# Pacing interleaved layer-0/1 steps by weights instead of by count, in a four-layer fp32 kernel

## The chip, the cores and the metric

The kernel runs on one core of a Trainium2 chip. The metric is the device time of one execution in microseconds (us), as the median of several runs. One further execution was recorded by the hardware profiler; all durations below are from that one.

## What is computed

The input is x of 16 batches, each 256 rows by 256 channels. Four layers are added to it one after the other (`x = x + layer(x)`), all in float32. Cut to what matters:

```python
# layer 0: gated exponential averages over the rows, 16 decays, then a gate, a product and a layer norm
ctx = causal_ema(x, tau_ctx)
gated = x * sigmoid(concat(x, ctx) @ Wg.T + bg)
mod = 0.5 + sigmoid(gelu(x @ Wn1.T + bn1) @ Wn2.T + bn2)         # one column per decay d
temporal = sum_d softmax(blend)[d] * causal_ema(gated * mod[d], tau_raws[d])
out = (gelu(x @ Wsoma.T + bsoma) * sigmoid(temporal @ Wtemp.T + btemp)) @ Wout.T
x = x + layernorm(out) * gamma + beta
# layer 1: masked softmax pooling over the rows
scores = tanh(x @ W1 + b1) @ v
x = x + (softmax(mask(scores)) @ x) / count
# layer 2: 8 experts and a shared one, every batch through all nine, hidden width 1024
x = x + sum_e coef[b, e] * ((silu(x @ Wg[e]) * (x @ Wu[e])) @ Wd[e])
# layer 3: an MLP of hidden width 1024 whose last 64 columns come from one of 8 experts
x = x + concat(gelu(x @ W1 + b1) @ W2 + b2, gelu(x @ W1 + b1) @ We[idx] + be[idx])
```

Matrix products keep float32 accuracy by splitting each operand into a rounded part and a low part, and adding three products: high x high, high x low, low x high (`mm3`, lines 95 to 98).

## The kernel before

**Layers 2 and 3 are the plan.** Lines 693 to 716 write a list `plan` of 640 units, of which 576 are layer-2 units and 64 are layer-3 units. A layer-2 unit (`l2_unit`, line 608) takes one chunk of 128 hidden columns of one expert for a pair of batches (512 columns), or two chunks for one batch (256 columns each). It does the products into pg and pu, Silu on ScalarE (line 595), the product with pu on VectorE (line 596), rounding on ScalarE and the low part on GpSimd (`hidden`), and two units later the product back into y (LAG is 2). Batch 0 goes alone through the first five experts (units 0 to 19), batch 1 joins at unit 20, batches 2 and 3 board at unit 56, and the later pairs at units 128, 200, 288, 360, 448 and 520. A layer-3 unit (`l3_chunk`, line 649) is shorter. In the planner's time, `at`, a layer-2 unit counts 4 and a layer-3 unit 3.

**Weights.** `prefetch` runs one load per chunk ahead, ten chunks at most (RING). The first two times that a chunk is used it comes raw from DRAM into one of two buffers (`raws`), ScalarE rounds it (line 542), VectorE or GpSimd makes the low part (line 544), and then the raw buffer is free for the next load. In the first five experts every third low part is GpSimd's, later all are VectorE's. From the third use on, the ready pair is read back from DRAM. All loads are issued in order by SyncE's queue.

**Layers 0 and 1 are woven in.** Each batch passes through two generators, which stop at each `yield`. `traces` (line 245) has 21 steps for a batch after the first:
- steps 0 to 3: the splits of x and the context scan; the small products; `mod` written to DRAM; and the gate (24 matmuls of 256 columns into a buffer of tag "ps", then two tanh)
- steps 4 to 19: one step for each of the 16 decays d (a "d-step" below): two products on VectorE (line 352), two scans on VectorE (line 356) and the sum into `tacc` on GpSimd (line 360); each second one loads two rows of `mod` (line 347). Step 9 also holds `soma`, 12 matmuls and two Gelu
- step 20: the split of the sum

`pooled` (line 385) has 10 steps: the gate on the traces (0), its product (1), the product with Wout and the norm (2, 3), transposes and the splits (4), scores (5, 6), the softmax (7), transposes of it (8), and the product pp with the sum into `acc` (9, lines 492 to 504). It is one serial chain over all engines. Outside batch 0, every product of both generators goes through the one buffer of tag "ps" in PSUM, so their order in the program is their order in time.

**The order.** `phases` (lines 740 to 753) says which generators run beside each other: pooled(b) beside traces(b+1). For b = 0 and odd b only FRONT = 4 steps of traces(b+1) are beside pooled(b), and the rest follows in a phase of its own. `feed` interleaves the generators of a phase in proportion to their steps. `due` (line 802) lists for each pair when its steps must be done (SLACK = 16 of `at` before it boards, about four units) and how many steps, `ready`, that is. After each unit, `pace` gives the steps per unit of `at` that meet the most urgent due time, `rate` is that times the unit's length, and lines 834 to 840 run as many whole steps as are owed. No step runs ahead of the first three units of a layer-3 group. Each step is placed behind the unit's product on VectorE and its last matmul (`step`, line 807); the program's compiler then orders each engine's queue by this order and by what it expects to be ready.

Of the kernel before, what the change touches and what calls it, by code (L numbers as in the profile page):

```python
# [19 lines left out]
ND = 16  # L20
# [3 lines left out]
FRONT = 4  # L24
# [5 lines left out]
LAG = 2  # L30
BOOST = 400
HOLD = 3
STEPS = {"traces": 21, "pooled": 10}
FIRST = 13
ALONE = 5
NEG = -1e30
# [8 lines left out]
def fused_kernel(  # L45
# [55 lines left out]
    def load_x(b):  # L101
        xr = xin.tile([P, 2, S], F32, tag="xr", name=f"xr{b}")
        nc.sync.dma_start(xr, xT[b])
        return xr

    def load_xt(b):
        xt = xin.tile([P, 2, S], F32, tag="xt", name=f"xt{b}", bufs=1)
        nc.sync.dma_start(xt, x[b])
        return xt
# [133 lines left out]
    held, last_of = {}, {}  # L243
# [364 lines left out]
    def l2_unit(pos, cis, bs):  # L608


        uid[0] += 1
        u = uid[0]
        n = S * len(bs)
        p = bs[0] // 2
        off = (bs[0] % 2) * S
        xt = x2_tiles[p]
        sl = slice(off, off + n)
        parts = [(ci, ring_tiles["e", pos, ci], slice(i * n, (i + 1) * n)) for i, ci in enumerate(cis)]
        pg = ps_gu.tile([P, 512], F32, tag="gu", name=f"pg_{u}")
        pu = ps_gu.tile([P, 512], F32, tag="gu", name=f"pu_{u}")  # L620
        for q, o in ((pg, 0), (pu, 256)):
            for _, w, cs in parts:
                for k in range(2):
                    ws = slice(o + k * P, o + (k + 1) * P)
                    mm3(q[:, cs], w[:, 0, ws], w[:, 1, ws], xt[:, 0, k, sl], xt[:, 1, k, sl], k == 0, k == 1)
        t = hidden(pg, pu, u)
        e = cis[0] // NF

        def down():
            if cis[0] % NF == 0:  # L630
                y_of[0] = [ps_y.tile([P, 512], F32, tag=f"y{m}", name=f"y{m}_{u}") for m in range(2)]
            for m in range(2):
                ws = slice(512 + m * P, 512 + (m + 1) * P)
                for ci, w, cs in parts:
                    mm3(
                        y_of[0][m][:, :n], w[:, 0, ws], w[:, 1, ws], t[:, 0, cs], t[:, 1, cs],
                        ci % NF == 0, ci % NF == NF - 1,
                    )
            if cis[-1] % NF == NF - 1:
                for m in range(2):  # L640
                    for i, b in enumerate(bs):
                        a = acc_of(b)[:, m]
                        V.scalar_tensor_tensor(  # L643
                            a, y_of[0][m][:, i * S : (i + 1) * S], coef[:, b, e : e + 1], a, ALU.mult, ALU.add
                        )
                if p in ends.get(pos, []) and bs[-1] % 2:
                    leaving.append(p)

        st2.push(down)

    def l3_chunk(p, f):
        uid[0] += 1
        xt = x2_tiles[p]
        w = ring_tiles[("f", p, f)]
        q = ps_gu.tile([P, 512], F32, tag="gu", name=f"q_{uid[0]}")
        for k in range(2):
            ws = slice(k * P, (k + 1) * P)
            mm3(q, w[:, 0, ws], w[:, 1, ws], xt[:, 0, k], xt[:, 1, k], k == 0, k == 1)
        t = hidden(q, None, uid[0], bias=vec[:, V_L3B1 + f : V_L3B1 + f + 1])
        u = uid[0]  # L660

        def down():
            if f == 0:
                y_of[0] = [ps_y.tile([P, 512], F32, tag=f"y{m}", name=f"z{m}_{u}") for m in range(2)]
            mm3(y_of[0][0], w[:, 0, 256:384], w[:, 1, 256:384], t[:, 0], t[:, 1], f == 0, f == NF - 1)
            for i in range(2):
                b = 2 * p + i
                cw = ring_tiles[("c", b, f // 4)]
                ws = slice((f % 4) * P, (f % 4 + 1) * P)
                ts = slice(i * S, (i + 1) * S)  # L670
                mm3(
                    y_of[0][1][:, ts], cw[:, 0, ws], cw[:, 1, ws], t[:, 0, ts], t[:, 1, ts],
                    f == 0 and i == 0, f == NF - 1 and i == 1, skip_group_check=True,
                )
            if f == NF - 1:
                a = acc_tiles[p]
                V.scalar_tensor_tensor(a[:, 0], y_of[0][0], vec[:, V_B2 : V_B2 + 1], a[:, 0], ALU.add, ALU.add)  # L677
                nc.sync.dma_start(out[p, :, 0], a[:, 0])
                for i in range(2):
                    b = 2 * p + i  # L680
                    ts = slice(i * S, (i + 1) * S)
                    V.scalar_tensor_tensor(  # L682
                        a[:, 1, ts], y_of[0][1][:, ts], bias3[:, b : b + 1], a[:, 1, ts], ALU.add, ALU.add
                    )
                nc.sync.dma_start(out[p, :, 1], a[:, 1])

        st2.push(down)
# [48 lines left out]

    n_done, n_steps = [0], [0]
    phases, alone, ready = [[(traces, 0)]], {}, []  # L740
    count = FIRST
    for b in range(NB):
        more = b + 1 < NB
        phases.append([(pooled, b)] + [(traces, b + 1)] * more)
        count += STEPS["pooled"]
        if more and (b == 0 or b % 2):
            alone[len(phases) - 1] = FRONT
            phases.append([(traces, b + 1)])
            ready.append(count + FRONT)
            count += STEPS["traces"]  # L750
        else:
            count += STEPS["traces"] * more
            ready.append(count)

    def feed():
        gens, left = {}, {}
        for i, phase in enumerate(phases):
            for f, b in phase:
                if f is traces and 0 < b + 1 < NB and b + 1 not in asked:
                    asked.add(b + 1)  # L760
                    xin_tiles[b + 1] = load_x(b + 1)
                    xt_tiles[b + 1] = load_xt(b + 1)
                if (f, b) not in gens:
                    gens[f, b] = f(b, b == 0)
                    left[f, b] = FIRST if (f, b) == (traces, 0) else STEPS[f.__name__]
            todo = {k: left[k] for k in phase}
            if i in alone:
                todo[phase[1]] = alone[i]
            total = sum(todo.values())
            share = {k: n / total for k, n in todo.items()}  # L770
            owed = dict.fromkeys(phase, 0.0)
            live = set(phase)
            while live:
                for k in phase:
                    owed[k] += share[k]
                k = max((k for k in phase if k in live), key=lambda k: owed[k])
                owed[k] -= 1
                todo[k] -= 1
                left[k] -= 1
                n_steps[0] += 1  # L780
                next(gens[k])
                if todo[k] == 0:
                    live.discard(k)
                if left[k] == 0:
                    assert next(gens[k], gens) is gens
                    n_done[0] += k[0] is pooled
                yield

    asked = set()
    steps = feed()  # L790
    while n_steps[0] < FIRST:
        next(steps)
# [6 lines left out]
    at = [0]  # L799
# [4 lines left out]
    def pace(t, s):  # L804
        return max([(s1 - s) / max(t1 - t, 1) for t1, s1 in due if s1 > s] or [1.0])

    def step():


        if "h" not in last_of:  # L810
            return next(steps, None)
        with tc.issue_after(last_of["h"].ins), tc.issue_after(last_of["pe"].ins):
            return next(steps, None)

    def leave():
        while leaving:
            split_x3(leaving.pop())

    owed = 0.0
    for i, item in enumerate(plan):  # L820
        kind, args, _, done = item[:4]
        if kind == "l2":
            bs = args[2]
            while n_done[0] <= bs[-1]:
                step()
            l2_unit(*args)
        else:
            if args[0] not in x3_done:
                st2.flush()
                leave()  # L830
            l3_chunk(*args)
        leave()

        rate = pace(at[i], n_steps[0]) * item[4]
        owed += rate
        soon = plan[min(i + 1, len(plan) - 1)]
        if not (soon[0] == "l3" and soon[1][1] < HOLD):
            for _ in range(min(int(owed), int(rate) + 2)):
                step()
                owed -= 1  # L840
        prefetch(len(done))
    st2.flush()

# [108 lines left out]
```

## Time and profile before

| | |
|---|---|
| median of 3 runs | 2860.03 us (2858.63 to 2860.83) |
| the profiled execution | 2858.32 us |
| its span, first to last instruction | 2856.1 us |
| TensorE busy (matmuls) | 2783.3 us, 97% |
| VectorE busy | 1440.9 us, 50% |
| GpSimd busy | 1294.4 us, 45% |
| ScalarE busy | 1238.7 us, 43% |

The profile's page shows busy time by engine, the span in 40 slices, and the costliest groups of instructions. In its lines, PE is TensorE, DVE VectorE, ACT ScalarE, POOL GpSimd, SP SyncE; "L352" is line 352 of the kernel; a group reads "output tile <- input tiles, shape, count". A view of waits names who waited, at which tile and line, for whom, with the sum, the count and the longest. A helper's line (L93 for a low part, L86 for a rounding on ScalarE, L96 to L98 for the three products) is shared by many tiles, so those groups are told apart by their tiles. Batch 0's layers 0 and 1 take the first 68 us; unit 0 starts at 68 us, and unit 56's first product at 402.65 us.

### The profile page before, as it was taken

Reading aid. Unit: us, or ns where it says so; the run is one execution under the profiler, and the core shown is the slowest. Engines: PE = TensorE matmul, PEld = TensorE weight load, DVE = VectorE, ACT = ScalarE, POOL = GpSimd, SP = SyncE. Lnnn points to the kernel's source line nnn. Section 1 sums busy time; section 2 is a strip of 40 time slices with the busy share of each in tenths; the row PEclk is TensorE's granted clock in tenths of the full one; section 3 lists DMA queues with packets and bytes.
Section 4 is the critical chain, followed back from the end, with each engine's and each line's share of the span. In section 5 each row is a group of like instructions: output and inputs, shape, how many; then the busy total and the mean of one; then the engine's idle time right before and its main releaser. Section 6 shows DMA issues by size and latency. Waiting matters only on the chain. (4 is left out here: it accounts for less than half of the span.)

```text
span 2856.1 us, 36960 instructions
## 1 busy us (share of the span) xinstructions
PE 2783.3 (97%) x13632; PEld 2338.7 (82%) x13632; DVE 1440.9 (50%) x2664; ACT 1238.7 (43%) x2054; POOL 1294.4 (45%) x981
## 2 busy tenths in 40 slices
PE   6899889999999999999999999999999999999999
PEld 3887678988888888888888888888888888888887
DVE  7878867665656454544545545444454542222222
ACT  5465555456444533435334443344433453233433
POOL 4655635544645453543535445344454443333333
PEclk8999999999999999999999999999999999999999
DMA  3344446547443442322433143332523243222552
GB/s 112 120 144 134 154 146 219 186 138 250 151 158 121 157 137 100 118 80 81 180 104 125 43 161 116 109 120 70 181 100 108 94 156 101 89 89 76 188 196 86
DMA packets 114694, 371.24 MB, mean 130 GB/s; under 512 B 12642, under 2 KB 30930, under 8 KB 114514
## 3 DMA queue, kind: packets, MB, share of 16 engines
q1 hardware_dynamic: 114514, 368.88, 38.8%
q8 instruction: 108, 1.77, 0.2%
q14 instruction: 72, 0.59, 0.1%
HBM read 304.62 MB, written 64.21 MB: 129 GB/s over the span
## 5 line engine op out<-in xcount | busy, mean ns | idle before, releaser
L93 POOL TENSOR_TENSOR hh<-h,hh 128x512 fp32r<-128x512 f32 x640 | 846.1, 1322 | 1339.2 <-ACT hh L86 1319.7
L596 DVE TENSOR_TENSOR h<-h,pu 128x512 f32<-128x512 f32 x576 | 393.8, 684 | 946.2 <-PE pu L98 823.0
L86 ACT ACTIVATE hh<-h 128x512 fp32r<-128x512 f32 x640 | 403.5, 631 | 936.7 <-DVE h L596 916.5
L96 PE MATMUL pg<-x,w_e 128*128 128x512 f32 (+1 forms) x1232 | 466.7, 379 | 12.9 <-ACT x L86 5.4
L595 ACT ACTIVATE h<-pg 128x512 f32<-128x512 f32 x576 | 342.8, 595 | 307.8 <-PE pg L98 228.8
L96 PE MATMUL pu<-x,w_e 128*128 128x512 f32 (+1 forms) x1232 | 464.9, 377 | 5.3 <-DVE h L596 2.8
L98 PE MATMUL pg<-x,w_e 128*128 128x512 f32 (+1 forms) x1232 | 465.3, 378 | 4.1 <-DVE w_e L93 3.3
L97 PE MATMUL y<-hh,w_e 128*128 128x512 f32 (+1 forms) x1232 | 464.3, 377 | 2.4 <-POOL hh L93 2.4
L97 PE MATMUL pg<-x,w_e 128*128 128x512 f32 (+1 forms) x1232 | 464.4, 377 | 0.4 <-POOL x L93 0.4
L98 PE MATMUL pu<-x,w_e 128*128 128x512 f32 (+1 forms) x1232 | 463.8, 376 | 0.0
L98 PE MATMUL y<-hh,w_e 128*128 128x512 f32 (+1 forms) x1232 | 463.6, 377 | 0.0
L97 PE MATMUL pu<-x,w_e 128*128 128x512 f32 (+1 forms) x1232 | 463.5, 376 | 0.0
L96 PE MATMUL y<-hh,w_e 128*128 128x512 f32 (+1 forms) x1232 | 415.7, 377 | 2.6 <-DVE acc L643 2.3
L360 POOL TENSOR_TENSOR ta<-ta,tr 128x512 f32<-128x512 f32 x225 | 309.7, 1376 | 70.0 <-DVE tr L356 59.3
L356 DVE TENSOR_TENSOR_SCAN tr<-decay,bt 128x256 f32<-128x256 f32 x450 | 284.4, 669 | 0.0
L96 PEld LDWEIGHTS pg<-x,w_e 128*128 128x128 f32 x1232 | 232.4, 189 | 57.4 <-ACT x L86 6.2
L96 PEld LDWEIGHTS pu<-x,w_e 128*128 128x128 f32 x1232 | 232.3, 189 | 48.8 <-DVE h L596 4.5
L98 PEld LDWEIGHTS pg<-x,w_e 128*128 128x128 f32 x1232 | 232.6, 189 | 47.9 <-DVE w_e L93 5.1
L97 PEld LDWEIGHTS y<-hh,w_e 128*128 128x128 f32 x1232 | 233.3, 189 | 46.1 <-POOL hh L93 4.5
L96 PEld LDWEIGHTS y<-hh,w_e 128*128 128x128 f32 x1232 | 231.6, 189 | 46.9 <-issue 2.9
L98 PEld LDWEIGHTS y<-hh,w_e 128*128 128x128 f32 x1232 | 233.3, 189 | 41.7
L98 PEld LDWEIGHTS pu<-x,w_e 128*128 128x128 f32 x1232 | 232.6, 189 | 42.0
(294 smaller groups left out, 3262.4 us busy)
## 6 DMA issues: line engine op xcount, KB each, us to landing
w_e<-keep_e SPq DMA_DIRECT2D x216, 768.0 KB, 4.3
raw_e<-in_wexp_dram SPq DMA_DIRECT2D x144, 384.0 KB, 4.3
keep_e<-w_e SPq DMA_DIRECT2D x72, 768.0 KB, 4.1
mod<-mdd SPq DMA_DIRECT2D x120, 256.0 KB, 3.8
w_f<-keep_f SPq DMA_DIRECT2D x56, 384.0 KB, 3.5
raw_c<-in_comb_dram SPq DMA_DIRECT2D x32, 260.0 KB, 2.8
xr<-in_xT_dram SPq DMA_DIRECT2D x16, 256.0 KB, 3.0
xt<-in_x_dram SPq DMA_DIRECT2D x16, 256.0 KB, 2.7
```

The source lines that it names most:

```text
L86: A.activation(out_, in_, AF.Copy)
L93: return (V if e == "v" else G).tensor_tensor(out_, in_, h.bitcast(F32), ALU.subtract)
L96: PE.matmul(o, wh, xh, start=start, stop=False, **kw)
L97: PE.matmul(o, wh, xl, start=False, stop=False, **kw)
L98: last_of["pe"] = PE.matmul(o, wl, xh, start=False, stop=stop, **kw)
L356: V.tensor_tensor_scan(tr[:, c], decay[:, d : d + 1].to_broadcast([P, S]), bt[:, c], 0.0, ALU.mult, ALU.add)
L360: G.tensor_tensor(tacc, tacc, tr, ALU.add)
L595: A.activation(h, ps_g, AF.Silu)
L596: last_of["h"] = V.tensor_tensor(h, h, ps_u, ALU.mult)
```

## The change

The steps get weights, listed in `STEPS`, in place of a count of one each: a d-step weighs 1.0, and the ten steps of `pooled` weigh 4.5 together. What is owed, what is ready and how far the work has come are all sums of these weights, and batch 0's first part no longer counts. At odd b, 12 steps of traces(b+1) instead of 4 run beside pooled(b) (BESIDE; b = 0 keeps FRONT). What a unit adds to the debt is at most 2.5, the debt is at most 4.0, and after a step of `pooled` no further step is placed behind the same unit.

```diff
-STEPS = {"traces": 21, "pooled": 10}
+STEPS = {
+    "traces": [0.9, 0.5, 0.1, 0.3] + [1.0] * ND + [0.3],
+    "pooled": [0.1, 0.6, 0.9, 0.5, 0.4, 0.3, 0.4, 0.5, 0.4, 0.4],
+}
+BESIDE = 12
...
-    n_done, n_steps = [0], [0]
+    n_done, n_steps, weight = [0], [0], [0.0]
     phases, alone, ready = [[(traces, 0)]], {}, []
-    count = FIRST
+    count = 0.0
     for b in range(NB):
         more = b + 1 < NB
         phases.append([(pooled, b)] + [(traces, b + 1)] * more)
-        count += STEPS["pooled"]
+        count += sum(STEPS["pooled"])
         if more and (b == 0 or b % 2):
-            alone[len(phases) - 1] = FRONT
+            n = alone[len(phases) - 1] = BESIDE if b else FRONT
             phases.append([(traces, b + 1)])
-            ready.append(count + FRONT)
-            count += STEPS["traces"]
+            ready.append(count + sum(STEPS["traces"][:n]))
+            count += sum(STEPS["traces"])
         else:
-            count += STEPS["traces"] * more
+            count += sum(STEPS["traces"]) * more
             ready.append(count)
...
                 todo[k] -= 1
+                if k != (traces, 0):
+                    weight[0] += STEPS[k[0].__name__][-left[k]]
                 left[k] -= 1
                 n_steps[0] += 1
+                last_of["part"] = k[0]
                 next(gens[k])
...
-        rate = pace(at[i], n_steps[0]) * item[4]
-        owed += rate
+        rate = pace(at[i], weight[0]) * item[4]
+        owed = min(owed + min(rate, 2.5), 4.0)
         soon = plan[min(i + 1, len(plan) - 1)]
         if not (soon[0] == "l3" and soon[1][1] < HOLD):
-            for _ in range(min(int(owed), int(rate) + 2)):
+            least = owed - rate - 1
+            while owed > max(least, 0.5) and weight[0] < count - 0.01:
+                was, last_of["part"] = weight[0], None
                 step()
-                owed -= 1
+                owed -= weight[0] - was
+                if last_of["part"] is pooled:
+
+                    break
         prefetch(len(done))
```

More of the change, by code (lines that the diff above doesn't have):

```diff
@@ L764, in feed @@
                     gens[f, b] = f(b, b == 0)
-                    left[f, b] = FIRST if (f, b) == (traces, 0) else STEPS[f.__name__]
+                    left[f, b] = FIRST if (f, b) == (traces, 0) else len(STEPS[f.__name__])
             todo = {k: left[k] for k in phase}
```

## The prediction

> **What bounds the kernel.** I read the page's 40 slices first: how full TensorE is, and where it is not.
>
> ```profile
> PE   6899889999999999999999999999999999999999
> DVE  7878867665656454544545545444454542222222
> PEclk8999999999999999999999999999999999999999
> ```
>
> A slice is 71.4 us. TensorE is full from the seventh slice on, so all that a reordering can win lies before about 410 us. The busy times by stretch say it in us (TensorE is the first pair behind the length, then its weight loads, VectorE, ScalarE, GpSimd):
>
> ```profile
> 68.00:129.00 61.00, 53.21 (x390) 50.39 (x391) 53.92 (x101) 28.42 (x47) 40.72 (x28) 0.95 0.40 118
> 129.00:193.00 64.00, 58.98 (x441) 55.77 (x440) 41.79 (x71) 41.35 (x68) 35.55 (x22) 0.96 0.50 152
> 193.00:350.00 157.00, 142.44 (x652) 112.42 (x652) 142.06 (x233) 85.70 (x137) 95.58 (x67) 0.99 0.44 135
> 350.00:410.00 60.00, 50.69 (x314) 45.86 (x313) 34.99 (x71) 27.97 (x50) 19.50 (x17) 0.91 0.48 158
> 410.00:2850.00 2440.00, 2434.85 (x11694) 2049.54 (x11694) 1117.47 (x2074) 1018.15 (x1679) 1068.77 (x819) 1.00 0.38 129
> ```
>
> Idle TensorE: 7.8, 5.0, 14.6 and 9.3 us in the four stretches from 68 to 410, then 5 us in all. By start-to-start times (0.227 us for 512 columns, 0.119 for 256 at the full clock; anything longer is a stall or a half clock) I get 14, 12, 23 and 15 us: 64 us that can be won at most. VectorE is 90% busy from 193 to 350, with 22.2 us idle before (129 to 193) and 25.0 us after (350 to 410). Two things bound the first stretches. The first is the chain of each `pooled`, which must end before its batch boards. The second is the loading loop of raw weights with two buffers: raw load, ScalarE's rounding, the low part, next load. The waits from 68 to 410 us show the loop:
>
> ```profile
> ACT w_e L86 <- DMA raw_e<-in_wexp_dram: 45.9, 33, 5.1
> DVE w_e L93 <- ACT w_e L86: 31.1, 22, 4.0
> ...
> PE pg L98 <- DVE w_e L93: 3.3, 4, 1.9
> ```
>
> ScalarE waits 45.9 us for raw chunks and VectorE 31.1 us for ScalarE. The view of tile raw_e gives the loop's pace: 10 issues from 92.0 to 127.5 (3.94 us each, VectorE beside it on batch 1's d-steps), 20 from 129.6 to 190.8 (3.22, few d-steps), 9 from 198.0 to 233.3 (4.41, batch 2's d-steps). So a d-step on VectorE slows the loop.
>
> The timeline before batch 2 and 3 board (unit 56, the first with both) shows the dearest place:
>
> ```profile
> 388.36 0.81 PE L486 MATMUL ppt<-ident,sc 128*128 128x128 f32 x4 [2.59 <-DVE sc L478]
> 391.06 0.55 PE L96 MATMUL pg<-x,wh 128*128 128x256 f32 x1 [1.90 <-DVE q L93]
> ...
> 396.10 0.41 PE L98 MATMUL pg<-c,wl 128*128 128x256 f32 x1
> 397.54 0.39 PE L498 MATMUL pp<-q,v 128*128 128x256 f32 x1 [1.02 <-ACT gp L299]
> ...
> 402.65 0.50 PE L96 MATMUL pg<-x,w_e 128*128 128x512 f32 x1 [3.42 <-ACT x L86]
> ```
>
> Unit 55 is done, and TensorE has only the end of pooled 3. Between its last two steps stand the 24 gate matmuls of traces 4: all use the one buffer of tag "ps", so pp waits until they and their tanh are through. They start 0.213 us apart, at half the clock.
>
> **Where the steps move.** I worked through both planners' arithmetic (rate = (ready - done)/(due - at) x 4). Due of batch 1 is 20 x 4 - 16 = 64. Before, 27 steps are done at unit 0 and ready is 58: 31/64 x 4 = 1.94 steps per unit. After, ready is 4.5 + 18.1 + 4.5 + 9.8 = 36.9 and 6.3 is done: 1.91 weights. Written t for `traces`, p for `pooled`, steps counted from 0, by unit:
> - p1.0 to p1.9: units 9 to 15 before, 9 to 18 after. Gate t2.3: 15 and 12. d-steps t2.4 to t2.10: 16 to 19 before, 13 to 18 after.
> - p2: 26 to 42 before, 25 to 40 after. p3: 44 to 51 and 41 to 50. Gate t4.3: 51 and 44. d-steps t4.4 to t4.11: 52 to 61 and 45 to 51.
> - p5 ends at 122 and 121, with five instead of seven of its steps left at the layer-3 units from 112. p15 starts at 501 and 507, ends at 515 and 516.
>
> No arithmetic goes or comes. Only places change, and each step takes its DMAs along.
>
> **Term 1: d-steps beside pooled 1.** A d-step is two products (0.41 us apart) and two scans (0.605 apart): 2.03 us of VectorE, plus one GpSimd sum of 1.38 and half a mod load. Seven of them, 14.2 us, move into a stretch where VectorE has 22.2 us free. So VectorE enters its 90% stretch 14.2 us ahead. But they slow the weight loop: 14 chunks (units 13 to 19). Bounds: nothing (3.22 us stays) and 14 x (4.41 - 3.22) = 17 us, the pace with batch 2's d-steps. The middle row, 3.94, had two d-steps per unit; here it is one, so I take half its excess: 14 x 0.36 = 5 us. Four mod loads move ahead of raw loads in SyncE's queue, with their wait for a free mod buffer (49.0 us over 19 waits from 68 to 410, longest 8.9); that is inside those bounds. Of the seven d-steps six have a GpSimd sum, which delays hh for two units' y; GpSimd is 56% busy there. Net lead: 14.2 - 5 = 9 us (-3 to 14), which pooled 2's end (352 us, in the VectorE-bound stretch) and so pooled 3's start get.
>
> Here a rule speaks against the change. Row: VectorE's low part of a chunk takes 0.93 us at best and up to 2.02 us (the tile view's 0.93, 0.96 median, 2.02); the longest, at 153.39, began 0.08 us after a GpSimd sum that ran to 154.60. The Trainium skill, "SBUF — State Buffer", section "Who interferes with whom": a VectorE instruction with two SBUF inputs and a GpSimd one that reads SBUF can't run together; the second waits out the first. By the rule, six more GpSimd sums could each hold a low part for up to 1.3 us, 8 us on the loop; by the median of the row almost none do, about 0. Neither changes the 5 us taken above.
>
> **Term 2: pooled 3.** From its tanh (358) to its last sum (402) it takes 44 us. The gate's leaving its tail frees 397.54 - 391.06 = 6.5 us; earlier it stands beside a VectorE-only step and full-clock unit work, where I charge 2 of its 24 x 0.119 = 2.9 us. Seven d-steps (14.2 us) now stand beside the chain, in a stretch with 25 us idle. The chain comes to VectorE some six times behind half a d-step: +6. The soma part (12 matmuls, 1.4 us) uses the same buffer: +1. Sum: -6.5 + 2 + 6 + 1 = +2.5 us, bounds -4.5 (no meeting) and +10 (a whole d-step each time).
>
> **Term 3: the clock.** If unit 55's end and the chain's end come closer, the first matmuls of unit 56 run at the full clock: the start-to-start excess right after 402.65 is 2.3 us. I take all of it (bounds 0 and 2.3).
>
> **Terms 4 and 5.** At 716 us the first matmul of unit 128 starts 1.4 us late, pooled 5 having ended at 715; with fewer steps left by then the stall goes: -1.4 (0 to -1.4). Pooled 15 ends its sum at 2367.5 and unit 520's Silu runs at 2378.0, so its first product is due near 2376. Its start moves six units later, three of them layer-3 units of some 2 us; from the unit where p15.2 was written (2322) its chain ran 45 us, two more steps need 7, and from 2325 that gives 2377, plus 2.5 for the split: 3 us late (0 to 8).
>
> **Sum.** -9 + 2.5 - 2.3 - 1.4 + 3 = -7.2 us. It is made against the profiled execution, 2858.32 us (span 2856.1, 2.2 us around it), which lies 1.7 us under the median 2860.03. Put on the median: **2852.8 us**.
>
> **Rivals.**
> - More is won: the loop keeps 3.22 us and the chain meets no d-step: -14.2 - 4.5 - 2.3 - 1.4 + 3 = -19.4, 2840.6 us. For it: 22 and 25 us of free VectorE. Against: the loop was slower in both stretches with d-steps. 0.14.
> - The written order hardly reaches the engines: p2.9 was written at unit 42 and ran at 49, so the lead may be used up by d-steps in front of pooled 3: -9 + 10 + 0 - 1.4 + 3 = +2.6, 2862.6 us, no change. 0.16.
> - **Slower:** the weight loop. Mod loads and low parts queue behind d-steps at units 13 to 19, and the loop takes the 4.41 us seen from 198 to 233. Unit 20 comes 17 us later, which is more than the lead: +2.8 + 2.5 + 0 - 1.4 + 3 = +6.9, 2867 us, more if unit 520's 8 us come too. It decides from a pace where 12.2 us are lost, 3.22 + 12.2/14 = 4.1 us per chunk. For it: both rows. Against: one low part in three is GpSimd's up to unit 19, and there is one d-step per unit. 0.30.
>
> **How the numbers follow.** The forecast has 0.40, and its own range is 2847 to 2858. About 0.2% (5.7 us) is what a measurement tells from no change. Faster: the first rival and 0.32 of the forecast, 0.46. Same: 0.08 of the forecast and the second rival, 0.24. Slower: 0.30. All the best bounds give -22.4, 2838; all the worst +20.8, 2881. The range 2838 to 2873 leaves out some 0.04 below and 0.14 above.
>
> **What would show it.** Term 1: VectorE busy over 50 of 64 us from 129 to 193, raw loads 3.6 us apart, unit 20 near 203. Term 2: pooled 3 starts near 349 and lasts 46 us; no gate matmul between ppt and pp; unit 56 near 396. Term 3: no half-clock row near it. Terms 4 and 5: no stall near 716, one of 3 us before unit 520. If raw loads go over 4.1 us, or TensorE's idle time before 410 us doesn't fall, the prediction is wrong.

## The result: 0.56% slower

| | median, us | runs |
|---|---|---|
| before | 2859.89 | 2858.32 to 2862.23 |
| after | 2875.64 | 2872.96 to 2879.24 |

The ratio is 1.0056, with a 95% interval of 1.0045 to 1.0067. The forecast was 2852.8 us, and the time lies above its range of 2838 to 2873. The span of the profiled execution grew from 2856.1 to 2874.1 us, by 18.0. The changed kernel's page, the same three rows of slices as before (a slice is 71.9 us now):

```profile
PE   6989979999999999999999999999999999999999
DVE  7878866656665454446344444444444442222222
PEclk8899979999999999999999999999999999999999
```

TensorE is full from the seventh slice on, as before; the sixth is new: 7 instead of 8, and at a lower clock. The busy times by stretch of the changed kernel (TensorE, its weight loads, VectorE, ScalarE, GpSimd; then clock, DMA share, GB/s):

```profile
68.00:129.00 61.00, 54.55 (x384) 52.27 (x384) 53.63 (x103) 28.53 (x46) 37.86 (x26) 0.88 0.39 127
129.00:193.00 64.00, 54.35 (x402) 50.52 (x403) 47.62 (x78) 42.26 (x67) 37.70 (x25) 0.97 0.45 137
193.00:350.00 157.00, 144.87 (x686) 114.92 (x686) 136.73 (x227) 84.90 (x136) 91.90 (x64) 1.00 0.44 136
350.00:410.00 60.00, 45.66 (x298) 41.66 (x296) 45.30 (x88) 27.41 (x48) 26.18 (x21) 0.86 0.57 188
410.00:430.00 20.00, 14.93 (x53) 11.72 (x54) 6.95 (x14) 5.82 (x10) 5.97 (x5) 0.64 0.05 13
```

By the excess of the start-to-start times, the stalls from 129 to 193 grew from 11.9 to 15.3 us, those from 193 to 350 fell from 23.3 to 20.1, and those from 350 to 430 grew from 14.9 to 28.1. The last is 13.2 of the 18 us. The clock of 0.64 from 410 to 430 is that of a TensorE that stands and starts again. The first Silu of unit 56, counted off in ScalarE's timeline, came at 407.9 us before and at 424.6 after: 16.7 us later.

Where it stands there shows in TensorE's waits of the changed kernel from 378 to 426 us (sum, times, longest):

```profile
PE psc L465 <- DVE ths L98: 5.3, 1, 5.3
PE pso L101 <- DVE mx L472: 3.7, 1, 3.7
PE pa L101 <- ACT x1T L452: 3.1, 1, 3.1
```

All three are steps of pooled 3 (psc and mx its scores and maximum, pa and x1T before them), or of traces 4 between them (pso). What VectorE did in that time, in its timeline:

```profile
396.13 2.43 DVE L361 TENSOR_TENSOR_SCAN tr<-decay,bt 128x256 f32<-128x256 f32 x4
398.46 2.43 DVE L357 SCALAR_TENSOR_TENSOR bt<-gp,bl,mod 128x256 f32<-128x256 f32 x6
400.80 0.69 DVE L361 TENSOR_TENSOR_SCAN tr<-decay,bt 128x256 f32<-128x256 f32 x1
401.52 0.42 DVE L98 TENSOR_TENSOR ths<-th,ths 64x256 fp32r<-64x256 f32 x1
401.97 3.02 DVE L361 TENSOR_TENSOR_SCAN tr<-decay,bt 128x256 f32<-128x256 f32 x5
404.90 0.85 DVE L357 SCALAR_TENSOR_TENSOR bt<-gp,bl,mod 128x256 f32<-128x256 f32 x2
405.67 0.42 DVE L472 CUSTOM_DVE_ANT_0 sc<-psc,mb 128x256 f32<-128x256 f32 x1
```

The line ths is one operation of 0.42 us of the chain that everyone waits for. Its input was rounded by 397.63; it starts at 401.52, behind four scans, six products and a scan of traces 4's d-steps, whose sum is first read at 456.8 us. The rounding on ScalarE in the changed kernel, and the same VectorE operation before, when VectorE stood waiting for its input:

```profile
397.21 0.42 ACT L91 ACTIVATE ths<-th 128x256 fp32r<-128x256 f32 x1
```

```profile
382.59 0.80 DVE L93 TENSOR_TENSOR ths<-th,ths 64x256 fp32r<-64x256 f32 x1 [1.51 <-ACT ths L86]
```

The same happens to the maximum (L472), behind five scans and two products. VectorE is busy, TensorE stands.

Pooled 3 by segments, each from the start of one operation to that of the next, in us, from the timelines. The first three columns are before, after and a run of the next section; the last is the run there with 1 instead of 4 steps beside pooled 3:

| pooled 3, from ... to | before | after | order only | 1 step at b = 3 |
|---|---|---|---|---|
| tanh of the gate (step 0) to the norm's statistics (2) | 7.0 | 16.0 | 16.1 | 7.6 |
| to x1 (3) | 2.4 | 2.3 | 2.3 | 2.9 |
| to the copy x1T (4) | 10.5 | 15.7 | 10.0 | 8.1 |
| to tanh of the scores (5) | 3.6 | 2.4 | 1.9 | 1.9 |
| to the maximum (6) | 4.4 | 9.0 | 6.0 | 4.1 |
| to the scaling (7) | 1.9 | 4.8 | 2.3 | 2.2 |
| to the sum into acc (9) | 13.3 | 7.4 | 10.5 | 5.6 |
| all | 43.1 | 57.6 | 49.1 | 32.4 |
| it started at | 358.1 | 360.3 | 360.5 | 358.4 |

The start is 2.2 us later, the chain 14.5 us longer: together the 16.7 us of unit 56.

### The profile page after: what moved, and what is told of

Its sections match the earlier page's. It is cut to its first block, busy times and chain, and to the rows that moved or that the text cites. A ratio compares the mean times of both kernels' runs of the same rounds, so it can differ in the third digit from the quotient of the medians.

```text
span 2874.1 us, 36938 instructions
## 1 busy us (share of the span) xinstructions
PE 2788.5 (97%) x13632; PEld 2340.3 (81%) x13632; DVE 1428.5 (50%) x2664; ACT 1239.5 (43%) x2052; POOL 1296.2 (45%) x981
```

## The experiments

Theory A: the loss is made beside pooled 3 alone, by the 12 steps of traces 4, whose d-steps fill VectorE's queue ahead of the chain's operations. Theory B: it starts at pooled 1; unit 20's Silu comes at 208.8 instead of 201.2 us (the weight loop's raw loads are 3.61 us apart from 130.0 to 191.3, 18 of them, instead of 3.22), and that lateness is handed on. Theory C: the limit of one pooled step per unit stretches the chains. Some expectations name a theory A2, formed after the first runs: the chain is lengthened by what shares its buffer as well as by what shares its queue. Ratios are to runs of the kernel before that were measured beside each run, with 95% intervals; "12 at b = 3" means 12 steps of traces(4) beside pooled(3).

### One place at a time, on the kernel before

```diff
-            alone[len(phases) - 1] = FRONT
+            n = alone[len(phases) - 1] = BESIDE.get(b, FRONT)
             phases.append([(traces, b + 1)])
-            ready.append(count + FRONT)
+            ready.append(count + n)
```

with `BESIDE = {3: 12}` in the first run and `{1: 12}` in the second.

> The kernel before, with one part of the change at one place: 12 instead of 4 steps of traces 4 beside pooled 3; counts, pace and everything else as before. Theory A (queue): traces 4's d-steps stand in VectorE's queue ahead of pooled 3's operations, pooled 3 lasts some 55 us instead of 44, unit 56 starts 10 to 17 us later, 2868 to 2877 us. Theory B (late start: unit 20 comes 8 us late because pooled 1 shares its units with traces 2, and that is passed on) and theory C (at most one step of pooled per unit stretches the chains): no change, 2857 to 2863 us.

Measured: 2876.22 us, ratio 1.0059 (1.0042 to 1.0076). Unit 20 at 201, pooled 3 from 358 to 418, unit 56 at 424. TensorE's waits from 378 to 426 us of this run:

```profile
PE psc L461 <- DVE ths L94: 5.3, 1, 5.3
PE ppt L487 <- DVE sc L479: 4.3, 2, 3.5
PE pso L97 <- DVE mx L468: 3.7, 1, 3.7
```

Two of the three rows are the changed kernel's to the digit. One number at one place, without weights, caps or limit, makes the whole loss.

> The kernel before, with 12 instead of 4 steps of traces 2 beside pooled 1 only. Theory B: unit 20 starts near 209 instead of 201 us, and the whole comes out 8 to 16 us later, 2868 to 2876. Theory A: unit 20 may come a few us later, but pooled 3 has no more d-steps beside it than before and unit 56 starts within 4 us of 402, 2856 to 2864 us. Theory C: no change.

Measured: 2861.73 us, ratio 1.0011 (1.0001 to 1.0021). Unit 20 came at 224.4 us, 23 later than before, three times the lateness of the changed kernel; yet unit 56 came at 411.5, 3.6 later. The busy times of this run, of the same columns as above:

```profile
129.00:193.00 64.00, 51.30 (x370) 48.67 (x371) 47.73 (x78) 34.16 (x55) 38.57 (x26) 0.93 0.46 143
193.00:350.00 157.00, 144.41 (x690) 118.88 (x689) 137.54 (x224) 87.93 (x142) 90.21 (x62) 0.94 0.39 120
350.00:410.00 60.00, 56.97 (x352) 51.48 (x351) 38.92 (x70) 33.93 (x58) 20.54 (x17) 0.97 0.64 207
```

TensorE idles 12.7 us from 129 to 193 instead of 5.0, and from 350 to 410 3.0 instead of 9.3: it had to wait there for pooled 3 anyway. Pooled 3 started at 350 here, 8 us sooner, and took 54.5 us, 11 longer, so that it ended 3 us later than before. Theory B falls: what is lost at unit 20 is nearly all forgiven at unit 56.

### The limit, and the weights alone

> The changed kernel without the rule of at most one pooled step per unit. Theory A2: traces 4 has the same steps beside pooled 3, so unit 56 stays near 425 and the time near 2873 to 2878 us; pooled 1 may end earlier, which unit 56 doesn't feel. Theory C (the rule stretches the chains): 2858 to 2866 us.

The edit takes out the two lines `if last_of["part"] is pooled: break`. Measured: 2876.18 us, ratio 1.0062 (1.0045 to 1.0079); unit 20 at 221, unit 56 at 429. Theory C falls.

> The changed kernel with 4 instead of 12 steps of the next traces beside each odd pooled, and without the rule of one pooled step per unit: what is left is the weights and the caps. Theory A: pooled 3 takes 44 us again and unit 56 starts between 395 and 405, 2850 to 2862 us. Theories B and C expect about the same, since what they blame is gone too. If it stays over 2868 us, the weights themselves are the cause.

The same with `BESIDE = 4`. Measured: 2885.22 us, ratio 1.0090 (1.0073 to 1.0107), a miss of every theory. Unit 56 came at 408.4, as before; the loss is later, 10 us of stalls from 650 to 800 us and 20 from 800 to 2350. TensorE's waits from 430 to 2350 us:

```profile
PE pg L101 <- ACT x L91: 8.3, 3, 3.4
PE pg L101 <- DVE q L98: 3.7, 2, 2.0
PE pp L503 <- ACT gp L304: 2.0, 2, 1.0
```

The first row is a unit that waits for its batch's x2, the last the gate in a pooled chain's tail. By the planner's arithmetic the ten steps of pooled weigh 4.5 and so are written late: p5 at units 114 to 123 instead of 101 to 121 in the changed kernel, and it ended at 723 us with unit 128 due. It looks as if the weights need the 12 steps beside, which count into what must be ready and so start pooled earlier; that reading was not tried by itself.

### VectorE's order alone

Each step stays where the changed kernel puts it; in `pooled` the last VectorE operation of a step is remembered as `last_of["pv"]`, and traces 4's VectorE operations are queued behind it:

```diff
-                next(gens[k])
+                behind = k == (traces, 4) and (pooled, 3) in live
+                with tc.issue_after(last_of["pv"].ins) if behind else nullcontext():
+                    next(gens[k])
```

> The changed kernel with every step in the same place of the plan; the only edit orders VectorE's queue: traces 4's operations are queued behind the last VectorE operation of pooled 3 written before them. Theory A: pooled 3's operations no longer wait behind d-steps, it takes 45 to 50 us, unit 56 starts 8 to 13 us earlier than in the changed kernel, 2861 to 2868 us. Theories B and C: nothing changes, 2873 to 2879 us.

Measured: 2866.65 us, ratio 1.0027 (1.0017 to 1.0036), 9 us below the changed kernel by the medians and 8 by the ratios. Pooled 3 took 49.1 us, unit 56 came at 416. VectorE's timeline of this run:

```profile
392.34 1.26 DVE L361 TENSOR_TENSOR_SCAN tr<-decay,bt 128x256 f32<-128x256 f32 x2
393.63 0.42 DVE L98 TENSOR_TENSOR ths<-th,ths 64x256 fp32r<-64x256 f32 x1
394.08 1.66 DVE L357 SCALAR_TENSOR_TENSOR bt<-gp,bl,mod 128x256 f32<-128x256 f32 x4
395.66 1.26 DVE L361 TENSOR_TENSOR_SCAN tr<-decay,bt 128x256 f32<-128x256 f32 x2
396.84 0.40 DVE L472 CUSTOM_DVE_ANT_0 sc<-psc,mb 128x256 f32<-128x256 f32 x1
```

Between ths and the maximum there are now four products and two scans, where there were two products and five scans, and ths, whose input was rounded by 391.75, waits 1.9 us instead of 3.9. The same work in another order is worth 8.5 of the chain's 14.5 us. The segment up to the norm, 16 us, is untouched: there no d-step had begun.

### What is left: the shared buffer

In that segment traces 4's products ph and pm and their ScalarE parts pass through the one buffer of tag "ps" between pooled 3's steps 0 and 2 (Gelu of ph at 366.3, tanh of pm at 371.2, the norm at 376.3). Before, they came between later steps (371.1 and 384.4).

> The changed kernel with VectorE's queue ordered as in the order-only run, and with the soma products of traces 4 at its d-step 12 instead of 5, so that they leave pooled 3's chain in the ps buffer. Theory A2: 3 to 5 us below the order-only run (2866.7), 2861 to 2864 us. If only VectorE's queue counted: the same as the order-only run.

The edit is `if d == (12 if b == 4 else 5)` ahead of `soma()`. Measured: 2869.05 us, ratio 1.0040 (1.0025 to 1.0054); pooled 3 took 48.9 us. Soma costs nothing; that part of the theory fell.

> The changed kernel with VectorE's queue ordered as in the order-only run (2866.7), and traces 4's products in the three buffers of the units' pg and pu instead of the one of tag ps. If the shared buffer holds pooled 3 up, above all before its norm (16 us there against 7 before the change), pooled 3 takes 38 to 43 us instead of 49 and the whole 2857 to 2862. If it is the place in TensorE's queue behind units, or anything else: 2864 to 2870.

Measured: 2855.99 us, ratio 0.9994 (0.9985 to 1.0004), some 10 us below the order-only run and 1 us below the range expected. The segment up to the norm fell from 16.1 to 7.9 us, as is expected if the shared buffer holds it up. But the whole chain took 47.3 us, not 38 to 43: it started at 344.7 instead of 360.5, pooled 2 having ended 13 us sooner, so that its later steps ran beside units of TensorE. From 350 to 410 us TensorE is nearly full:

```profile
350.00:410.00 60.00, 58.58 (x358) 52.09 (x357) 50.11 (x99) 32.15 (x55) 37.44 (x28) 1.00 0.63 206
```

So with the other buffer the rest of the loss is gone, but what of the gain is the shorter segment and what the earlier end of pooled 2, whose compiled order changed too, isn't told apart. That the buffer alone made the rest is not shown.

### Fewer steps instead of more

> The kernel before with 1 instead of 4 steps of traces 4 beside pooled 3, so that none of traces 4's products stands between pooled 3's in the buffer of tag ps. Theory A2 (the chain is lengthened by what shares its buffer and its queue): pooled 3 takes 31 to 36 us instead of 43, unit 56's Silu comes at 398 to 403 instead of 408, 2848 to 2854 us. Rival (unit 56 is late because pooled 2 and the VectorE-bound stretch end late): pooled 3 is no faster end to end, 2857 to 2862.

The kernel before with `BESIDE = {3: 1}`. Measured: 2850.55 us, ratio 0.9975 (0.9966 to 0.9985). Pooled 3 took 32.4 us (last column of the table), unit 56 came at 397.6. Its stretch:

```profile
350.00:410.00 60.00, 56.11 (x347) 50.51 (x346) 30.41 (x58) 29.68 (x53) 19.47 (x15) 0.94 0.44 147
```

VectorE is busy 30.4 us here, 35.0 before and 45.3 after the change; TensorE 56.1, 50.7 and 45.7. VectorE's load is not the measure by itself: the run with the other buffer has 50.1 us of VectorE there and 58.6 of TensorE. With 1 step, traces 4's later products leave pooled 3's buffer as well as its queue, so this run doesn't tell the two apart.

> The kernel before with 1 instead of 4 steps of the next traces beside every odd pooled. Theory A2: pooled 1 ends earlier, but traces 2 starts later in the VectorE-bound stretch, so pooled 3 starts up to 8 us later; unit 56 between 396 and 410, 2847 to 2861 us; the later boards keep their slack. Rival as in the run with one place: 2858 or later.

`{b: 1 for b in range(1, 16, 2)}`. Measured: 2854.90 us, ratio 0.9992 (0.9983 to 1.0002). Pooled 3 took 26 us, but started at 368, as traces 2 began later; unit 56 at 400.7.

> The kernel before with 8 instead of 4 steps of traces 2 beside pooled 1, and 1 instead of 4 of traces 4 beside pooled 3. If the two findings add (d-steps done beside pooled 1 let pooled 3 start earlier; nothing of traces 4 in pooled 3's way makes it short), pooled 3 starts near 354 and unit 56's Silu comes at 393 to 396: 2846 to 2850 us, 1 to 4 below the run with 1 at pooled 3 alone (2850.6). If unit 20's lateness counts instead, TensorE ends unit 55 too late: 2850 to 2856.

Measured: 2848.96 us, ratio 0.9969 (0.9957 to 0.9981). Pooled 3 from 347 to 389, unit 56 at 394.5. Time and unit 56 are as expected, though pooled 3 started 7 us sooner than expected and took 42 us instead of the 32.4 of the run with 1 at b = 3 alone; by their intervals the two times aren't told apart.

> The changed kernel without the limit of one pooled step per unit and with 1 instead of 12 steps of traces 4 beside pooled 3; the weights, the caps and the 12 steps at the other odd batches stay. If the one place beside pooled 3 is all that the change costs, unit 56 comes at 396 to 405 and the time is 2846 to 2858. If the weights cost something by themselves, the time stays over 2860.

The changed kernel without the limit, with `(1 if b == 3 else BESIDE) if b else FRONT`. Measured: 2846.56 us, ratio 0.9960 (0.9945 to 0.9975): the best, faster than both kernels. Unit 20 at 218, unit 56 at 391.4. Its busy times:

```profile
129.00:193.00 64.00, 51.36 (x373) 48.42 (x372) 48.09 (x79) 34.45 (x55) 38.07 (x26) 0.93 0.45 145
193.00:350.00 157.00, 149.09 (x742) 125.01 (x742) 138.33 (x227) 92.17 (x151) 95.98 (x65) 0.99 0.44 141
350.00:410.00 60.00, 58.02 (x360) 51.69 (x360) 36.76 (x69) 35.10 (x58) 21.99 (x17) 1.00 0.49 167
```

Beside the run without the limit (2876.18) it differs in one number, 1 for 12 at b = 3: 29.6 us.

> The run with the weights, no limit and 1 step beside pooled 3 (2846.6 us), with 8 instead of 12 steps of traces 2 beside pooled 1. There unit 20 came at 218 us and TensorE lost 20 us from 129 to 193. If that lateness reaches unit 56: unit 20 near 210, unit 56 near 388, 2842 to 2846 us. If the VectorE-bound stretch behind it decides, fewer d-steps done early give it back: unit 56 at 391 or later, 2846 to 2850 us.

Measured: 2849.09 us, ratio 0.9962 (0.9948 to 0.9975), the same as the run above. Unit 20 came at 213, 5 us sooner, and unit 56 at 392.9: unit 20's lateness doesn't decide. Nor does the length of pooled 3 alone: with more steps beside pooled 1 it started 8 to 11 us sooner, and part of that was lost to a longer chain (54.5 instead of 43.1 us with 12 at b = 1, 42.0 instead of 32.4 with 8 at b = 1 and 1 at b = 3). What unit 56 waits for is its end.

## Why the prediction was wrong, step by step

**Reading what bounds it** was right: all of the difference but some 3 us arises before 430 us, and 13.2 us of it at the place that was named as the dearest, pooled 3 before unit 56. (The 3 us are two new stalls, 1.0 us at 1363 and 1.9 us at 1669, for which the prediction had no term.) Terms 1 and 2 are the steps that failed: together they were forecast as -6.5 us and came to +16.7. The prediction's own sign of being wrong showed, too: TensorE's idle time from 68 to 410 us rose from 36.7 to 42.6 us.

**Term 1** said that pooled 3 would start 9 us sooner; it started 2.2 us later. The half on the weight loop held: raw loads 3.61 us apart were forecast as 3.6, and unit 20 came 7.6 us late where 5 were taken. The other half failed by a count. The plan moves seven d-steps to units 13 to 18, but the kernel before writes the same seven at units 16 to 19. VectorE was busy 47.6 us of the 64 from 129 to 193, not over 50; at unit 20's Silu it had done the scans of nine d-steps of traces 2, against five before. That is a lead of four, 4 x 2.03 = 8.1 us, and 7.6 us of late units eat it: the last scan of traces 2 starts at 232 instead of 234 us. Also, "VectorE-bound from 193 to 350" was an average. VectorE has a gap in it in both kernels; the first of these rows is before, the second after:

```profile
232.00:275.00 43.00, 41.17 (x201) 33.03 (x200) 33.13 (x45) 27.25 (x44) 17.94 (x12) 1.00 0.49 145
```

```profile
232.00:275.00 43.00, 40.55 (x198) 32.39 (x197) 33.03 (x47) 26.82 (x44) 16.28 (x11) 1.00 0.50 152
```

Ten us are free there in each, between the end of traces 2 and the first d-step of traces 3, whose first steps and pooled 2's share the ps buffer. How much of a larger lead passes this gap stays open: with 12 steps beside pooled 1 alone, pooled 3 started 8 us sooner (349.7), and with the weights and without the limit 1 us sooner (357.2).

**Term 2** said +2.5 us for pooled 3; it was +14.5. The gate's leaving the tail gave 13.3 - 7.4 = 5.9 us, forecast 6.5. "The chain comes to VectorE some six times behind half a d-step: +6" failed. The queue holds d-steps in bunches (six products, then the scans), so ths alone waited 3.9 us; the order-only run wins back 8.5 us, with some d-steps still in between. "I charge 2" for the gate's earlier place failed too: the charge overlooked that ph and pm move along, to a place where each stands in TensorE's queue behind units' products (pm's input was ready at 367.7 and pm began at 370.1; the buffer was free at 371.6 and the next product of pooled 3 began at 374.0). The segment up to the norm grew by 9.0 us. Soma, charged with 1, cost nothing. The bound of +10 didn't cover this, and by the prediction's own terms a whole d-step at each of six meetings makes 12.2 - 6.5 + 2 + 1 = 8.7, not 10. (The plan before also has t4.11 at unit 60, not 61; nothing rests on that.)

**Term 3**, 2.3 us for the full clock, needed the gap before unit 56 to close; it grew, and the clock from 410 to 430 was 0.64. **Term 4**: the stall of 1.4 us at 716 went, and one of 1.4 came at 702: 0 instead of -1.4. **Term 5**: a stall of 0.7 us before unit 520, not 3; pooled 15 ended at 2395, unit 520's Silu came at 2399.

**The rivals.** The time is nearest the slower one, but its mechanism was wrong: it set the loss at the weight loop, and the loop did slow, only to 3.61 us, and 23 us of lateness at unit 20 came to 3.6 at unit 56 where 12 steps stood beside pooled 1 alone. The second rival had the right place, d-steps ahead of pooled 3 at 10 us, and was given no change, since the 9 us of term 1 paid for it.

The rule on the port that VectorE and GpSimd share (the Trainium skill, "SBUF — State Buffer", section "Who interferes with whom") was weighed at 0 to 8 us. The median low part of a raw chunk from 129 to 193 us rose from 0.96 to 1.10 us, in the direction that it says; on 13 of them that is 2 us, and part of the slower loop at most.

## What to carry to other kernels

An engine's idle time beside a serial chain is not free to fill: filler that is ready early stands in the engine's queue in front of the next short operation that everyone waits for (here 0.42 us of work waited 3.9 us behind eleven operations). Look for what the whole machine waits for when the filler would run, and put filler beside chains whose lateness is made good later (pooled 1 here: 23 us at unit 20, 3.5 in the whole), not beside the one that ends last (pooled 3). Work moved earlier is a lead only by what is done at the next meeting point more than before, and a buffer that two chains share is worth a look, too: with another buffer one segment fell from 16.1 to 7.9 us, though that run doesn't set the buffer's part of the gain apart.

## What the runs showed of the hardware

TensorE's half clock is a cost of its own at such a place. In the changed kernel the granted clock was 0.86 from 350 to 410 us and 0.64 from 410 to 430, and 1.00 from 350 to 410 in the best run, where TensorE didn't stand. In the changed kernel's pooled 3, 256-column matmuls started 0.213 us apart at 395 us, with a granted clock of 0.50 from 394 to 398, and 0.119 apart at 359 us, with 1.00 from 358 to 361. And in the run with 12 steps beside pooled 1, 7.7 us more of idle TensorE from 129 to 193 us was made good by 410 us (2.0 us less from 193 to 350, 6.3 less from 350 to 410), because a wait was there in any case.
